# Counting four of sixteen key chunks earlier, adding six groups beside the slots, and two stores on another queue

## The chip, the cores and the metric

The kernel runs on one core of a Trainium2 chip. The metric is the device time of one execution in microseconds (us). The core has TensorE (PE, with its weight loads as PEld), VectorE (DVE), ScalarE (ACT), GpSimd (POOL) and SyncE (SP), each with its own queue of instructions that it works off in order; DMAs are issued from such a queue.

## The reference

Two layers work on 8192 nodes (128 graphs of 64) with 256 features.

```
x = x + L0_gnn(layernorm(x), adj)     # softplus(xn @ W_self + (I - A_norm) @ xn @ W_neigh)
x = x + L0_ffn(layernorm(x))          # H = gelu(xf @ W1 + b1): 8192 x 1024
                                      # probs = softmax(H @ Wg + bg); e = argmax(probs)
                                      # out = probs[e] * (H @ Wd[e] + bd[e]): one of 8 experts per node
x = x + L1_gnn(layernorm(x), adj)     # attention in each graph, layernorm, gelu
x = x + L1_ffn(layernorm(x), edges)   # messages over 1048576 edges give scores; two of 4 experts per node
```

The edge list's indices run up to 65536, but there are only 8192 nodes: a source past the last node is read as the last node, and edges whose target is past the last node do not count. So most edges that count have the last node as source, and for these it is enough to know how many go to each node (`cnt`). The others are collected as keys and handled one by one.

## The kernel before

Nodes lie in 64 tiles of 128; four tiles make a group (`GR`), two groups a part (`PART`). The program is written as generators: each `yield` ends a step, and `mix` (L168) interleaves several generators by the share of their steps that is done. A planner puts the instructions on the engines' queues by its own model of their times, with the written order as priority; so an instruction without a wait can be placed long before the place where it is written. `tc.issue_after(i)` keeps instructions behind `i` on its engine.

**Gate stage** (loop over i = 0 to 9 at L935 on). Streams of part i: `factors`, `graph` (layer 0's graph for two groups, i < 8), `gated` (L707; layer 0's hidden layer, the gate and the choice of an expert for two groups, i >= 2) and `keys.collect` (L259; for some chunks of 512 edges per partition it takes the largest keys with MAX8 and MATCH_REPLACE8 on DVE and stores the rest to `left`). `gated` sends each node's row of the hidden layer to `hrows`, sorted by expert, with indirect DMAs from GpSimd (L800). At i = 9 `early_table` finds eight tiles of `hrows` that are already full.

**Early slots** (`early_slots`, L859). For those eight tiles SP loads the hidden rows, PE transposes them and multiplies by the expert's weights `wd` (L914), DVE adds the bias (L922), and SP stores the result to `yrows` (L923). `slot_tables` (L978) is stepped beside them; it gives the tables by which the next stage finds its tiles.

**Slots** (`slots`, L1162; the loop at L1273 on). 60 further tiles are done in the same manner: `hin` loaded by SP (L1194), eight transposes to `th` (L1203), copied to `hTt` by ACT (L1206), sixteen matmuls to `py` (L1221), bias on DVE (L1229), store by SP (L1230). Each slot also steps three generators, issued after the slot before:

- `count` (L306): for a chunk's 96 keys per partition DVE splits the bits (`pi`, `pb`: L314, L316), makes one-hots for 16 keys (`HK`) with `pairs_equal` (L201; 128 and 64 wide, bf16), and PE sums their products in `cnt_ps`, one matmul per key (L326). Sixteen chunks of six steps make 96 steps.
- `finish` (L335): DVE finds each list's inner edges and writes the sorted keys (`own`, `pieces`, `key_tile`, `key_row`).
- `back_first` (L1139): for the first four groups (`FIRST` = 2 * `PART`) GpSimd gathers a tile's rows of `yrows` as soon as they are all stored (L1149), DVE adds them to `x` and takes the statistics (L1156, L1157), and `factors_of` makes the factors of the layernorm.

What is left of the three generators runs after the last slot, and then a branch (L1285) jumps over four further slots that these inputs do not need.

**Graph stage of layer 1** (loop over s = 4 to 25, L1604). In step s `back(s)` (L1434) gathers and adds group s like `back_first`, `first(s - 4)` starts a group's attention (z on ACT or DVE at L1329 and L1331, transposes at L1471), `second`, `combine` and `tables` follow some steps later, and from the later steps on units of the last feed-forward (`dense`) are put between.

Memory pools of one stage are laid over those of the stage before; a new tile waits for the old tile's last reader.

Of the kernel before, what the change touches and what calls it, by code (L numbers as in the profile page):

```python
# [21 lines left out]
P = 128  # L22
# [10 lines left out]
NSLOT = 72  # L33
SURE = 68
EARLY = 8
EPS = 1e-5
NEG = -9000000000000000.0
HALVES = (slice(0, 64), slice(64, 128))
# [44 lines left out]
def kernel(  # L83
# [113 lines left out]
    def pairs_equal(pool, numbers, of, k, n, name):  # L197
# [8 lines left out]
        )  # L206
        return o

    sorted_keys = {}
    facs = {}  # L210

# [14 lines left out]
    class Keys:  # L226
# [76 lines left out]
                keys.rearrange("p (n e) -> p n e", e=PER),  # L303
            )

        def count(self):  # L306

            behind = []
            for c in range(n_chunks):
                bits = self.slots.bitcast(I32)[:, c * KEPT : c * KEPT + KEPT]  # L310
                part = []
                for op, by, off in ((ALU.bitwise_and, P - 1, 0.0), (ALU.logical_shift_right, 7, -float(KEY >> 7))):
                    pi = self.work.tile([P, KEPT], I32, name="pi")
                    V.tensor_scalar(pi, bits, by, None, op)  # L314
                    pb = self.work.tile([P, KEPT], BF16, name=f"pb{by}")
                    V.tensor_scalar(pb, pi, off, None, ALU.add)  # L316
                    part.append(pb)
                for g in range(0, KEPT, HK):
                    one = []
                    for wi, pb, n in ((self.iota[0], part[0], P), (self.iota[1], part[1], NT)):  # L320
                        one.append(pairs_equal(self.twice, wi, pb[:, g : g + HK], HK, n, f"one{n}"))
                    behind.append((c * KEPT + g, one))
                    yield
                    at, one = behind.pop(0)
                    for k in range(HK):
                        nc.tensor.matmul(  # L326
                            self.ps,
                            one[0][:, k // 2, :, k % 2],
                            one[1][:, k // 2, :, k % 2],
                            start=(at + k == 0),  # L330
                            stop=(at + k == n_chunks * KEPT - 1),
                        )
            V.tensor_copy(cnt, self.ps)

        def finish(self, pool):  # L335

# [100 lines left out]
    with tc.tile_pool(name="w0", bufs=1, reuse_waits="tile") as w0, tc.tile_pool(name="kp", bufs=1, reuse_waits="tile") as kp:  # L437
# [30 lines left out]
        with tc.tile_pool(name="bg1", bufs=1, reuse_waits="tile") as bg1, tc.tile_pool(  # L468
# [19 lines left out]
            with tc.tile_pool(name="b2", bufs=1, reuse_waits="tile") as b2, tc.tile_pool(  # L488
# [370 lines left out]
                def early_slots():  # L859

                    _, rows_at = nc.values_load_multi_w_load_instructions(
                        early_row,
                        engines=(mybir.EngineType.SP,),
                        min_val=0,
                        max_val=E0 * N - P,
                        skip_runtime_bounds_check_because=why,
                    )
                    _, ex = nc.values_load_multi_w_load_instructions(
                        early_e,
                        engines=(mybir.EngineType.SP, mybir.EngineType.PE),  # L870
                        min_val=0,
                        max_val=E0 - 1,
                        skip_runtime_bounds_check_because=why,
                    )
# [24 lines left out]
                    load(1)  # L899
                    turn(0)  # L900
                    yield
                    for t in range(EARLY):
                        if t + 2 < EARLY:
                            load(t + 2)
                        if t + 2 == EARLY:
                            y_last = bh.tile([P, GR * P], F32, name="hT")[:, 0:D]
                        if t + 1 < EARLY:
                            turn(t + 1)
                        hT = turned_.pop(t)
                        bd = b2.tile([P, D], F32, name=f"z{2 + t % 2}")  # L910
# [12 lines left out]
                        nc.sync.dma_start(yrows[(NSLOT + t) * P : (NSLOT + t + 1) * P, :], y)  # L923
                        yield

                next_found(-1)
# [8 lines left out]
                for i in range(n_parts + 2):  # L935
# [25 lines left out]
                    if i >= 2:  # L961
                        with tc.issue_after(gelus[-1]) if gelus else ExitStack():
                            for at in islice(zeros, 2):
# [1 line left out]
                                    yrows[at : at + 8 * P, :].rearrange("(p r) (k f) -> p (r k) f", r=8, f=P),  # L965
                                    none.unsqueeze(1).to_broadcast([P, 8 * D // P, P]),
                                )
                    cs = [next(chunks) for _ in range((0, 1, 1, 2, 1, 2, 1, 2, 3, 3)[i])]
                    if cs:
                        streams.append((chain(*map(keys.collect, cs)), 8 * len(cs)))  # L970
                    if i == n_parts + 1:
                        streams.append((early_table(), 8))
                    mix(streams)
# [134 lines left out]
                early = early_slots()  # L1108
                for _ in early:
                    next(tables, None)  # L1110
                for _ in tables:
                    pass

        keep = ctx.enter_context(tc.tile_pool(name="keep", bufs=1, side="right", reuse_waits="tile"))
        sorted_keys["pieces"] = keep.tile([P, NB, PL, NPC], BF16, name="pieces")
# [3 lines left out]
        if True:  # L1119
            with tc.tile_pool(name="bs", bufs=3, reuse_waits="tile") as bs, tc.tile_pool(  # L1120
# [10 lines left out]
                keys.ps = psl.tile([P, NT], F32, name="cnt_ps")  # L1131
                steps, counts = keys.finish(bm), keys.count()
                stores, gathers = [], []

                def apart(made, others):
# [2 lines left out]

                def back_first():  # L1139

                    fac = None
                    for t in range(FIRST * GR):
                        i = t % (PART * GR)
                        if i == 0:
                            raw, fac = raws1[t // (PART * GR)], facs[t // (PART * GR)]
# [5 lines left out]
                        )  # L1151
                        gathers.append(got.ins)
                        apart(got, stores[t + E0 :])
                        for _ in range(3):
                            yield
                        V.scalar_tensor_tensor(x[:, t, :], y, psel[:, t : t + 1], x[:, t, :], ALU.mult, ALU.add)  # L1156
                        V.bn_stats(raw[:, 0, i, :], x[:, t, :])  # L1157
                        if i == PART * GR - 1:
                            yield
                            facs["last"] = factors_of(raw, None, [m[:, None, :] for m in mfs], fac)  # L1160

                def slots(first, end):  # L1162

# [100 lines left out]
                        )  # L1264
                    yield

                raws1 = [c0.tile([P, 1, PART * GR, 6], F32, name=f"raw_{i}") for i in range(FIRST // PART)]
# [4 lines left out]
                for t, unit in enumerate(slots(0, SURE - EARLY)):  # L1272
                    done = t  # L1273
                    with tc.issue_after(last) if last is not None else ExitStack():
                        next(back_early, None)
                        next(counts, None)
                        next(counts if t % 2 else steps, None)
                    if t >= SURE - EARLY - 8:
                        next(more, None)
                    last = unit  # L1280
# [129 lines left out]
    with ExitStack() as of_c:  # L1410
# [193 lines left out]
        for s in range(FIRST, n_steps):  # L1604
            if s % PART == 0:
                made["raw"] = c2.tile([P, 3, PART * GR, 6], F32, name="raw")
                made["eps"] = c2.tile([P, 3, PART * GR], F32, name="eps")
                V.memset(made["raw"], 0.0)
                V.memset(made["eps"], EPS)
            streams = []  # L1610
            for of, by_steps in ((back, 0), (combine, COMBINE), (tables, TABLES), (second, SECOND), (first, FIRST)):
                if 0 <= s - by_steps < NG:
                    streams.append((of(s - by_steps), 2 if of == second and s % 2 else 0))
            if s == TABLES + 1:
                with tc.issue_after(made["sent"]):
# [822 lines left out]
```

## Time and profile before

| | us |
|---|---|
| median of 3 runs | 2006.49 (2000.83 to 2007.28) |
| the profiled execution | 2002.07 |
| its span, first to last instruction | 2000.4 |
| PE busy (10609 matmuls) | 1875.0 (94%) |
| DVE busy | 1345.0 (67%) |
| ACT busy | 949.7 (47%) |
| POOL busy | 447.0 (22%) |

All times of the profile count from the span's start. In its tables a line gives the kernel's line, the engine, the operation and the tiles (written <- read). A wait names the engine and line whose end released the waiting instruction, with its total, the number of times and the longest. The mean granted clock of TensorE was 0.977 of full speed.

The stages lie so: gate to 616, early slots to 655, slots from 663 to 969, graph stage of layer 1 from 987 to about 1340, edges and the last feed-forward after it.

### The profile page before, as it was taken

To read this page: it belongs to the slowest core of one execution; us is meant where nothing else is said; L and a number is where in the kernel's file an instruction comes from. 1 tells how busy PE (TensorE), PEld (TensorE's weight loads), DVE (VectorE), ACT (ScalarE), POOL (GpSimd) and SP (SyncE) were. 2 spreads that over 40 slices of the span, in tenths; PEclk is the share of its full clock that TensorE was granted. 3 is DMA by queue.
4 is the path that set the end of the run, shared out by engine and by line. 5 is a ranking of instruction groups with operands and counts; after the bars stand their busy time and mean duration, and the time that the engine had idled before them with its cause. 6 is when DMAs were issued, how large, how long until landed. Compare 5 with 4: busy or idle time off the path is not lost. (4 is left out here: it accounts for less than half of the span.)

```text
span 2000.4 us, 32559 instructions
## 1 busy us (share of the span) xinstructions
PE 1875.0 (94%) x10609; PEld 1334.1 (67%) x10609; DVE 1345.0 (67%) x4421; ACT 949.7 (47%) x1740; POOL 447.0 (22%) x465
## 2 busy tenths in 40 slices
PE   7898999989999899999787999998999989999999
PEld 5444454544447899898654766665777758888876
DVE  6789988872224788999898775766788552334435
ACT  4867667676663121222277677432343423433332
POOL 2010111011110011100232100014677643313223
PEclk9999999999999999999897999998999999999999
DMA  9752322323425455554214211382322258888832
GB/s 295 209 164 81 119 83 97 109 90 113 157 94 170 166 169 172 167 163 144 69 53 158 76 50 53 111 246 67 74 51 68 83 178 286 286 250 280 278 122 95
DMA packets 243743, 284.91 MB, mean 142 GB/s; under 512 B 55920, under 2 KB 195568, under 8 KB 243568
## 3 DMA queue, kind: packets, MB, share of 16 engines
q1 hardware_dynamic: 209680, 222.22, 35.4%
q0 software_dynamic: 23040, 60.22, 9.2%
q8 instruction: 90, 1.47, 0.3%
q10 hardware_dynamic: 10848, 0.30, 0.3%
q14 instruction: 85, 0.70, 0.1%
HBM read 159.40 MB, written 123.18 MB: 141 GB/s over the span
## 5 line engine op out<-in xcount | busy, mean ns | idle before, releaser
L480 PE MATMUL ph<-zT,w 128*128 128x512 f32 x512 | 250.2, 613 | 4.2 <-ACT zT L729 3.2
L1221 PE MATMUL py<-wd,hTt 128*128 x960 | 217.6, 380 | 0.0
L1221 PEld LDWEIGHTS py<-wd,hTt 128*128 128x128 f32 x960 | 178.1, 191 | 22.6 <-issue 0.8
L1832 POOL DMA_INDIRECT got<-tsrc,esrc x144 | 156.1, 1084 | 157.6 <-DMA zslots<-none 75.6
L1206 ACT COPY hTt<-th 128x512 f32<-128x512 f32 x120 | 64.6, 589 | 248.0 <-PE th L1203 248.0
L1371 PE MATMUL py<-w,hT 128*128 128x256 f32 x736 | 173.3, 388 | 8.1 <-DVE kt L1771 4.7
L1361 PE MATMUL ph<-zT,w 128*128 128x512 f32 x368 | 168.1, 599 | 0.0
L480 PEld LDWEIGHTS ph<-zT,w 128*128 128x128 f32 x512 | 94.2, 196 | 107.0 <-issue 87.6
L1371 PEld LDWEIGHTS py<-w,hT 128*128 128x128 f32 x736 | 138.6, 193 | 34.2 <-issue 10.4
L2317 ACT ACTIVATE hT<-ph,b1e 128x256 f32<-128x256 f32 x152 | 72.1, 474 | 177.7 <-PE ph L2313 97.3
L2313 PE MATMUL ph<-zTp,w1e 128*128 128x256 f32 x608 | 139.3, 383 | 4.4 <-DMA w1e<-in_L_ffn_W_dram 4.4
L1365 ACT ACTIVATE hT<-ph,b 128x512 f32<-128x512 f32 x92 | 63.1, 688 | 163.3 <-PE ph L1361 161.6
L800 POOL DMA_INDIRECT hrows<-rows,pos x64 | 64.5, 1007 | 333.7 <-issue 160.4
L2334 DVE TENSOR_TENSOR y<-py,b2e 128x256 f32<-128x256 f32 x76 | 32.2, 424 | 158.6 <-PE py L2326 153.4
L2326 PE MATMUL py<-w,hT 128*128 x608 | 137.5, 379 | 0.0
L2313 PEld LDWEIGHTS ph<-zTp,w1e 128*128 128x128 f32 x608 | 116.7, 192 | 20.7 <-issue 4.6
L642 PE MATMUL pre<-wd 128*128 128x512 f32 x256 | 125.4, 607 | 1.9 <-ACT wd L628 1.3
L483 ACT ACTIVATE hT<-ph,b 128x512 f32<-128x512 f32 x128 | 88.1, 688 | 74.1 <-PE ph L480 72.5
L2326 PEld LDWEIGHTS py<-w,hT 128*128 128x128 f32 x608 | 112.6, 190 | 13.8
L201 DVE TENSOR_TENSOR one<-iota_l,pb 128x2048 bf16<-128x2048 bf16 x96 | 116.6, 1214 | 0.0
L1361 PEld LDWEIGHTS ph<-zT,w 128*128 128x128 f32 x368 | 67.2, 190 | 66.9 <-issue 66.0
L2347 POOL DMA_INDIRECT back<-yslots,place x64 | 65.2, 1019 | 165.9 <-ACT yb L1387 48.9
(486 smaller groups left out, 3799.6 us busy)
## 6 DMA issues: line engine op xcount, KB each, us to landing
hin<-hrows SPq DMA_DIRECT2D x60, 512.0 KB
w1e<-in_L_ffn_W_dram SPq DMA_DIRECT2D x38, 512.0 KB
yin<-ystore SPq DMA_DIRECT2D x24, 512.0 KB
yrows<-none SPq DMA_DIRECT2D x10, 1024.0 KB
zslots<-none SPq DMA_DIRECT2D x38, 256.0 KB
zin<-zslots SPq DMA_DIRECT2D x38, 256.0 KB
yslots<-y SPq DMA_DIRECT2D x76, 128.0 KB
ystore<-y SPq DMA_DIRECT2D x72, 128.0 KB
```

The costliest lines, as they stand in the source:

```text
L201: V.tensor_tensor(o, numbers.unsqueeze(1).to_broadcast(shape), of.rearrange("p (j e) -> p j e", e=2).unsqueeze(2).to_broadcast(shape), ALU ...
L480: nc.tensor.matmul(ph, w1[:, c, q * P : q * P + P], zT[:, c, :], start=(c == 0), stop=(c == 1))
L483: gelus.append(S.activation(hT, ph, AF.Gelu, bias=b1[:, q : q + 1]).ins)
L642: nc.tensor.matmul(pre, xnT[:, c, n * P : n * P + P], wcat[:, c, :], start=(c == 0), stop=(c == 1),)
L1221: nc.tensor.matmul(py, hT[:, q, :], wd[:, bass.ds(e, 1), q, :].rearrange("p e f -> p (e f)"), start=(q == 0), stop=(q == NH - 1),)
L1361: nc.tensor.matmul(ph, w1[:, e, c, q * P : q * P + P], zT[:, c, :], start=(c == 0), stop=(c == 1))
L1371: nc.tensor.matmul(py, hTs[q][:, k * P : k * P + P], w2[:, e, q, :], start=(q == 0), stop=(q == NH1 - 1))
L1832: nc.gpsimd.indirect_dma_start(got, None, tsrc, bass.IndirectOffsetOnAxis(ap=esrc[:, b, at : at + 1], axis=0))
L2313: nc.tensor.matmul(ph, w1e[:, c, q * P : q * P + P], zT[:, c, :], start=(c == 0), stop=(c == 1))
L2317: pace[:] = [S, S.activation(hT, ph, AF.Gelu, bias=b1e[:, q : q + 1]).ins]
L2326: nc.tensor.matmul(py, hTs[q][:, k * P : k * P + P], w2[:, e, q, :].rearrange("p e f -> p (e f)"), start=(q == 0), stop=(q == NH1 - 1),)
L2347: nc.gpsimd.indirect_dma_start(got[n], None, yslots[h], bass.IndirectOffsetOnAxis(ap=place[h][:, j, t : t + 1], axis=0))
```

## The change

- `count` takes a range of chunks, the number of keys in a step and its PSUM tile. Chunks 0 to 3 (`COUNTED`) are counted in steps of 8 keys (`HE`) as a stream of the gate stage at i = 8 and 9 (18 steps in each) and beside the early slots (two steps for each early tile). Their working tiles are carved (`Carved`) from those of `collect` and from factors no longer used. The other 12 chunks are counted in the slots as before, and the two sums are added. Bits are split in two halves of 48 keys, in a smaller tile `pi`.
- The collects are written earlier: 0, 1, 2, 2, 2, 3, 3, 3 chunks in parts 0 to 7 and none after, where it was 0, 1, 1, 2, 1, 2, 1, 2, 3, 3.
- In the slots `count` gets five steps in four slots (six before), `finish` five in eight (four before).
- `back_first` adds six groups (`BACKED`), with two steps for a tile in place of three; the addition comes one tile behind the gather. The graph stage's `back` skips groups 4 and 5, and copies their statistics.
- The last two of the eight early stores are issued by GpSimd.

```diff
+BACKED = 3 * PART
+COUNTED, HE = 4, 8
...
-        def count(self):
-            behind = []
-            for c in range(n_chunks):
+        def count(self, cs, hk, ps):
+            first, end = cs[0] * KEPT, (cs[-1] + 1) * KEPT
+            for c in cs:
...
-                    pi = self.work.tile([P, KEPT], I32, name="pi")
-                    V.tensor_scalar(pi, bits, by, None, op)
                     pb = self.work.tile([P, KEPT], BF16, name=f"pb{by}")
-                    V.tensor_scalar(pb, pi, off, None, ALU.add)
+                    for g in range(0, KEPT, KEPT // 2):
+                        pi = self.work.tile([P, KEPT // 2], I32, name="pi")
+                        V.tensor_scalar(pi, bits[:, g : g + KEPT // 2], by, None, op)
+                        V.tensor_scalar(pb[:, g : g + KEPT // 2], pi, off, None, ALU.add)
...
-                for g in range(0, KEPT, HK):
+                for g in range(0, KEPT, hk):
...
-            V.tensor_copy(cnt, self.ps)
+            if first:
+                V.tensor_tensor(cnt, cnt, ps, ALU.add)
+            else:
+                V.tensor_copy(cnt, ps)
...
-                        nc.sync.dma_start(yrows[(NSLOT + t) * P : (NSLOT + t + 1) * P, :], y)
+                        queue = nc.sync if t < EARLY - 2 else nc.gpsimd
+                        queue.dma_start(yrows[(NSLOT + t) * P : (NSLOT + t + 1) * P, :], y)
...
-                    cs = [next(chunks) for _ in range((0, 1, 1, 2, 1, 2, 1, 2, 3, 3)[i])]
+                    cs = [next(chunks) for _ in range((0, 1, 2, 2, 2, 3, 3, 3, 0, 0)[i])]
...
+                    if i == n_parts:
+                        l, r = (keys.work.tile([P, CHUNK], I32, name=n).bitcast(BF16) for n in ("src", "dst"))
+                        m = keys.work.tile([P, CHUNK + PER], F32, name="key").bitcast(BF16)
+                        n = HE * NT
+                        keys.work = keys.twice = Carved(
+                            one128=(l, r),
+                            one64=(m[:, 0:n], m[:, n : 2 * n]),
...
+                            pi=(gone[:, P : P + KEPT // 2].bitcast(I32),),
+                        )
+                        counts = keys.count(range(COUNTED), HE, psa.tile([P, 2 * D], F32, name="pre")[:, 0:NT])
+                    if i >= n_parts:
+                        n = COUNTED * (KEPT // HE) * 3 // 8
+                        streams.append((islice(counts, n), n))
...
                 for _ in early:
                     next(tables, None)
-                for _ in tables:
-                    pass
+                    next(counts, None)
+                    next(counts, None)
+                for of in (tables, counts):
+                    for _ in of:
+                        pass
...
-                steps, counts = keys.finish(bm), keys.count()
+                steps = keys.finish(bm)
+                counts = keys.count(range(COUNTED, n_chunks), HK, psl.tile([P, NT], F32, name="cnt_ps"))
...
-                    for t in range(FIRST * GR):
+                    for t in range(BACKED * GR):
...
-                        for _ in range(3):
-                            yield
-                        V.scalar_tensor_tensor(x[:, t, :], y, psel[:, t : t + 1], x[:, t, :], ALU.mult, ALU.add)
-                        V.bn_stats(raw[:, 0, i, :], x[:, t, :])
+                        yield
+                        if held:
+                            add()
+                        held.append((t, y))
+                        yield
...
-                        next(counts if t % 2 else steps, None)
+                        next(steps if t % 2 == 0 or t % 8 == 3 else counts if t % 4 == 1 else iter(()), None)
...
+                if s < BACKED:
+                    V.tensor_copy(made["raw"][:, 0], raws1[s // PART][:, 0])
...
-                if 0 <= s - by_steps < NG:
+                if 0 <= s - by_steps < NG and (of != back or s >= BACKED):
```

More of the change, by code (lines that the diff above doesn't have):

```diff
@@ L207, in pairs_equal, with __init__, tile @@
         return o
+    class Carved:
+        def __init__(self, **views):
+            self.views, self.at = views, dict.fromkeys(views, 0)
+        def tile(self, shape, dtype, name):
+            views = self.views[name]
+            self.at[name] += 1
+            view = views[self.at[name] % len(views)]
+            if len(shape) == 4:
+                return view.rearrange("p (j n e) -> p j n e", n=shape[2], e=2)
+            return view
     sorted_keys = {}
@@ L312, in count @@
                 for op, by, off in ((ALU.bitwise_and, P - 1, 0.0), (ALU.logical_shift_right, 7, -float(KEY >> 7))):
-                    pi = self.work.tile([P, KEPT], I32, name="pi")
-                    V.tensor_scalar(pi, bits, by, None, op)
                     pb = self.work.tile([P, KEPT], BF16, name=f"pb{by}")
-                    V.tensor_scalar(pb, pi, off, None, ALU.add)
+                    for g in range(0, KEPT, KEPT // 2):
+                        pi = self.work.tile([P, KEPT // 2], I32, name="pi")
+                        V.tensor_scalar(pi, bits[:, g : g + KEPT // 2], by, None, op)
+                        V.tensor_scalar(pb[:, g : g + KEPT // 2], pi, off, None, ALU.add)
                     part.append(pb)
-                for g in range(0, KEPT, HK):
+                for g in range(0, KEPT, hk):
                     one = []
                     for wi, pb, n in ((self.iota[0], part[0], P), (self.iota[1], part[1], NT)):
-                        one.append(pairs_equal(self.twice, wi, pb[:, g : g + HK], HK, n, f"one{n}"))
-                    behind.append((c * KEPT + g, one))
+                        one.append(pairs_equal(self.twice, wi, pb[:, g : g + hk], hk, n, f"one{n}"))
                     yield
-                    at, one = behind.pop(0)
-                    for k in range(HK):
+                    at = c * KEPT + g
+                    for k in range(hk):
                         nc.tensor.matmul(
-                            self.ps,
+                            ps,
                             one[0][:, k // 2, :, k % 2],
                             one[1][:, k // 2, :, k % 2],
-                            start=(at + k == 0),
-                            stop=(at + k == n_chunks * KEPT - 1),
-                        )
-            V.tensor_copy(cnt, self.ps)
+                            start=(at + k == first),
+                            stop=(at + k == end - 1),
+                        )
+            if first:
+                V.tensor_tensor(cnt, cnt, ps, ALU.add)
+            else:
+                V.tensor_copy(cnt, ps)
         def finish(self, pool):
@@ L967 @@
                                 )
-                    cs = [next(chunks) for _ in range((0, 1, 1, 2, 1, 2, 1, 2, 3, 3)[i])]
+                    cs = [next(chunks) for _ in range((0, 1, 2, 2, 2, 3, 3, 3, 0, 0)[i])]
                     if cs:
                         streams.append((chain(*map(keys.collect, cs)), 8 * len(cs)))
+                    if i == n_parts:
[5 more added lines that the diff above has]
+                            one64=(m[:, 0:n], m[:, n : 2 * n]),
+                            pb127=(m[:, 2 * n : 2 * n + KEPT],),
+                            pb7=(m[:, 2 * n + KEPT : 2 * n + 2 * KEPT],),
+                            pi=(gone[:, P : P + KEPT // 2].bitcast(I32),),
[4 more added lines that the diff above has]
+                        streams.append((islice(counts, n), n))
                     if i == n_parts + 1:
@@ L1130 @@
                 keys.psum, psl = pool("psp", 1, space=PSUM), pool("psl", 1, space=PSUM)
-                keys.ps = psl.tile([P, NT], F32, name="cnt_ps")
-                steps, counts = keys.finish(bm), keys.count()
+                steps = keys.finish(bm)
+                counts = keys.count(range(COUNTED, n_chunks), HK, psl.tile([P, NT], F32, name="cnt_ps"))
                 stores, gathers = [], []
@@ L1139, in back_first, with add @@
                 def back_first():
-                    fac = None
-                    for t in range(FIRST * GR):
-                        i = t % (PART * GR)
-                        if i == 0:
-                            raw, fac = raws1[t // (PART * GR)], facs[t // (PART * GR)]
+                    held = []
+                    def add():
+                        t, y = held.pop()
+                        i, part = t % (PART * GR), t // (PART * GR)
+                        raw = raws1[part]
+                        V.scalar_tensor_tensor(x[:, t, :], y, psel[:, t : t + 1], x[:, t, :], ALU.mult, ALU.add)
+                        V.bn_stats(raw[:, 0, i, :], x[:, t, :])
+                        if i == PART * GR - 1 and part in facs:
+                            facs["last"] = factors_of(raw, None, [m[:, None, :] for m in mfs], facs[part])
+                    for t in range(BACKED * GR):
                         while done < t + E0 - 1:
@@ L1153, in back_first @@
                         apart(got, stores[t + E0 :])
-                        for _ in range(3):
-                            yield
-                        V.scalar_tensor_tensor(x[:, t, :], y, psel[:, t : t + 1], x[:, t, :], ALU.mult, ALU.add)
-                        V.bn_stats(raw[:, 0, i, :], x[:, t, :])
-                        if i == PART * GR - 1:
-                            yield
-                            facs["last"] = factors_of(raw, None, [m[:, None, :] for m in mfs], fac)
+                        yield
[3 more added lines that the diff above has]
+                        yield
+                    yield
+                    add()
                 def slots(first, end):
@@ L1265, in weights @@
                     yield
-                raws1 = [c0.tile([P, 1, PART * GR, 6], F32, name=f"raw_{i}") for i in range(FIRST // PART)]
+                raws1 = [c0.tile([P, 1, PART * GR, 6], F32, name=f"raw_{i}") for i in range(BACKED // PART)]
                 for i in range(FIRST // PART):
```

## The prediction

> **What bounds the kernel now.** I read the page first for the shares, then the table of stages (busy time of each engine in chosen stretches), the order in time of PE, ACT, SP and DVE around the seams that the table shows, and last the waits there.
>
> ```profile
> span 2000.4 us, 32559 instructions
> 508.00:613.00 105.00, 96.58 (x400) 49.44 (x400) 24.42 (x129) 65.41 (x105) 15.93 (x16) 0.95 0.35 127
> ...
> 655.00:663.00 8.00, 3.14 (x15) 3.17 (x16) 6.94 (x30) 1.48 (x3) 0.00 (x0) 0.64 0.68 237
> 663.00:969.00 306.00, 303.72 (x2829) 273.01 (x2828) 272.74 (x627) 63.13 (x118) 25.22 (x16) 1.00 0.49 158
> 969.00:988.00 19.00, 8.07 (x144) 7.60 (x141) 18.51 (x39) 6.12 (x12) 2.46 (x1) 0.65 0.16 47
> 988.00:1020.00 32.00, 31.07 (x145) 21.48 (x143) 25.63 (x86) 18.37 (x44) 18.11 (x19) 0.94 0.24 71
> 1020.00:1060.00 40.00, 27.75 (x111) 18.06 (x110) 37.68 (x123) 28.62 (x52) 16.99 (x17) 0.83 0.19 56
> ```
>
> The columns after the length are busy PE, weight load, DVE, ACT and POOL, then granted clock, DMA share, GB/s. PE is full in the slots (663 to 969), and DVE with 272.7 of 306 close behind. In the gate's last groups (508 to 613) DVE works 24 of 105 us. Two holes are plain: 655 to 663, and 969 to 988, where DVE is full and PE works 8 of 19 us at a clock of 0.65. From 1020 to 1060 DVE (37.7 of 40) holds PE up again. From 1100 to 1300 PE has over 49 of every 50 us, so time won before it should last to the end.
>
> PE's order of time in the slots, at their end, and the waits from 940 to 1000:
>
> ```profile
> 667.15 1.04 PE L1203 MATMUL th<-ident,hin 128*128 128x128 f32 x8
> 668.02 3.62 PE L1221 MATMUL py<-wd,hTt 128*128 x16
> 671.48 1.13 PE L326 MATMUL cnt_ps<-one,one 128*128 128x64 bf16 x32
> ...
> 968.74 1.13 PE L326 MATMUL cnt_ps<-one,one 128*128 128x64 bf16 x32
> ...
> 986.67 1.01 PE L326 MATMUL cnt_ps<-one,one 128*128 128x64 bf16 x16 [0.73 <-DVE one L201]
> 987.49 1.95 PE L1471 MATMUL tz<-ident,z 128*128 128x128 f32 x8
> ...
> ACT z L1329 <- PEq L1285: 10.9, 1, 10.9
> ACT z L1329 <- DVE pieces L434: 8.4, 1, 8.4
> ```
>
> The last slot's matmuls end at 968.7; next comes counting, paced by DVE's one-hots, until 986.7, and only then the first transpose of the graph stage. Its input, ACT's z, waited for PE's branch and for DVE's last step of `finish`.
>
> SP's order at the other seam, and PE's row that waits there:
>
> ```profile
> 651.86 0.35 SPq L923 DMA_DIRECT2D yrows<-z  x1
> 655.36 0.35 SPq L923 DMA_DIRECT2D yrows<-hT  x1
> 656.54 1.41 SPq L1194 DMA_DIRECT2D hin<-hrows  x3
> ...
> 659.86 3.65 PE L1203 MATMUL th<-ident,hin 128*128 128x128 f32 x16 [5.04 <-DMA hin<-hrows]
> ```
>
> SP issues in order, so the slots' first loads stand behind the last early store, which waits for PE's last early tile.
>
> **The change, part by part.** Minus is time saved.
>
> *Counting moved.* 96 steps of 16 keys make 1536 matmuls; a quarter, 384, leaves. Two slots take 10.14 us (667.15 to 677.29) with 48 count matmuls; two pure slots are 2 x (0.87 + 3.46) = 8.66, so a count matmul costs 1.48/48 = 31 ns. Before, 1536 - 144 = 1392 (87 steps) lay in the slots; after, at most 72 steps do: 15 x 0.48 = **-7.2 us**. The 384 go beside the gate and the early slots as 48 steps of 8 keys: 384 x 31 ns = 11.9 us of PE. PE idles 8.4 of 105 us in 508 to 613, one wait of 1.4 us in each group (for ACT's row copies) among it; the planner can put counting there. I fill 4 us: **+7.5**, bounds +3 (all 8.4 filled) and +12. On DVE a step costs 0.68 (1024 elements, as the row of 128x1024) plus about 0.42 (512 elements, estimated on the line through 1214 ns for 2048 and 682 for 1024): 48 x 1.1 = 53 us. DVE is idle for 81 us in 508 to 613 and for 16 in 616 to 655, which hides it if the plan puts the one-hots ahead of their matmuls; the uncovered price is in the second rival. The collects were planned for later parts, yet the last MAX8 of a chunk ran at 428 us, so dealing them out earlier costs nothing (if DVE pushed the graph's work back there, up to +3).
>
> *The end of the slots.* Count steps are now offered 60 + 15 = 75 times in 60 slots, for 73 needed; `finish`, with some 33 steps, gets 38 places (30 before); the 24 gathered tiles need 7 + 2 x 24 = 55 slots. So all three should end inside. Does DVE hold it? From 655 to 988 it worked 6.9 + 272.7 + 18.5 = 298. Off: 24 steps at 1.75 (42) and four chunks of split bits (2). On: the split in halves of 12 chunks (6), eight more tiles at 0.47 + 0.42 less overlap (6.5). That is 267 of the 300 us or so from the last early tile to the end of the slots: 89%, as before, and at that share PE waited only 1.6 us for one-hots in the whole stage. What remains at 968.7 to 987.5 (18.7 us) is PE's branch, four z (2.1 us, 972.17 on) and the hand-over, some 3.5 us: **-15.2**, bounds -8 (half the tail stays) and -16.5.
>
> *Clock.* With the hole PE restarts slowly: eight transposes take 1.95 us at 987.49 and 1.09 at 995.94, eight matmuls of 257 columns 3.22 and 2.00. **-2** (0 to -3). [...]
>
> *Six groups beside the slots.* Eight tiles leave the graph stage: 8 x (0.47 + 0.42) = 7.1 us of DVE and eight gathers on POOL. DVE holds PE only from 1020 to 1060, where PE idles 12 us: I take **-4** (0 to -7). A copy of statistics comes on DVE, under 0.3 us.
>
> *Two stores to GpSimd.* SP is free after its last bias load at 648.06; register reads (0.8 us) and the three loads follow, and land by about 654, 3.3 us after issue as now. PE then goes on at 655 instead of 659.86 and skips part of the slow restart (3.65 for 16 transposes against 2 x 1.04). In exchange GpSimd's two stores land later than SP's: its nearest rows are gathers, 0.95 to 1.69 us of issue and 4.6 us to landing, and the first copy to hTt may wait for the buffer of the sixth store, about 0.5 us. POOL's queue is empty there until the first gather at 705. **-5** (-7 to +1).
>
> [...]
>
> *Sum:* -7.2 + 7.5 - 15.2 - 2 - 4 - 5 = -25.9. Against the profiled execution's 2002.1 us that is 1976.2; against the median shown, 2006.5 (4.4 above that execution), 1980.6. I put it halfway, 1978.
>
> **The rivals.**
> 1. *Part of the tail stays*: DVE falls behind in the slots, whose in-order queue is 89% full, and `finish` or the counts run past the last slot. For: PE waits for one-hots at 947 and 959, when the weights' few steps come on top. Price: half of the 18.7 us and PE stalls of 2: 1978 + 10 = 1988.
> 2. *The gate pays (slower)*: PE's queue is in order, so a count matmul planned too early for its one-hot stops all gate matmuls behind it. A step fully exposed costs 1.1 us, 48 of them 53, in place of the +7.5: 2004 - 33 (the sum without the +7.5) + 12 + 53 = 2036. It decides from (26 + 6)/48 = 0.67 us of stall a step. Against it: DVE is 77% idle there, two pairs of buffers let it run ahead, and in the slots a DVE three times as busy did not stop PE.
> 3. *Given back later*: the graph stage starts 26 us earlier but is held by its own chain (z, exp, ring on ACT and DVE, PE 27.8 of 40 us) and the replanned order is worse by as much: no change, 2004. Against: PE is full from 1100, so only a 100 us stretch could swallow it.
> 4. *The stores do nothing*: the loads still wait, for a buffer instead of SP. Then the -5 becomes 0: 1983, inside the forecast's range.
>
> **How the numbers follow.** Forecast (with the fourth) 0.63, first rival 0.17, second 0.10, third 0.10. The forecast's own range from the bounds, not all met at once, is 1966 to 1992. The first rival lies within it and up to 1998, where I put the end; the slow case and most of "given back" stay outside. A measurement here can tell about 0.3% (6 us) from no change. Faster 0.81 (forecast and first rival with a little of the third), same 0.08, slower 0.11.
>
> **What would show it.** Right: count matmuls (form 128x64, bf16) between 500 and 655, none after the last slot's py; under 5 us from that py to the first graph transpose, and no stretch there at 0.65 clock; hin issued before the last early y; 5 count steps in each 4 slots; 40 gathers in the graph stage. Wrong: PE waits for DVE's one-hots between 500 and 655 of over 10 us in all, group periods in the gate over 30 us (25 now, 2 more expected), `finish` steps after the last py, or a longer stretch from the first graph transpose to 1100's full PE.

## The result, and the profile after

The changed kernel takes 1975.58 us (median of 6 runs, 1971.18 to 1977.13); the kernel before, in 6 runs beside them, 2003.05 us (2000.42 to 2007.28). The ratio is 0.9856, with a 95% interval of 0.9839 to 0.9874: faster by 1.4%. The forecast was 1978. The profiled execution took 1972.22 us with a span of 1970.5, against 2002.07 and 2000.4 before.

The table of stages of the changed kernel (start and end, length, then busy PE, weight load, DVE, ACT and POOL, the granted clock, DMA share, GB/s):

```profile
508.00:613.00 105.00, 98.26 (x656) 56.07 (x655) 52.81 (x210) 65.46 (x105) 16.42 (x16) 1.00 0.35 128
657.00:660.40 3.40, 2.16 (x17) 1.75 (x17) 3.04 (x19) 0.67 (x2) 0.63 (x1) 1.00 0.97 368
660.40:959.00 298.60, 295.50 (x2577) 264.87 (x2577) 266.83 (x669) 63.66 (x119) 38.97 (x24) 1.00 0.52 167
959.00:961.00 2.00, 1.01 (x6) 0.47 (x6) 0.97 (x4) 1.71 (x4) 0.00 (x0) 1.00 0.22 70
960.05:992.05 32.00, 30.44 (x145) 20.53 (x146) 20.03 (x74) 23.24 (x55) 11.14 (x12) 1.00 0.20 55
992.00:1032.00 40.00, 26.87 (x113) 17.36 (x111) 38.32 (x126) 29.72 (x54) 17.95 (x17) 0.83 0.20 60
```

Three things are to be seen. In the same 105 us of the gate PE now holds 656 instructions in place of 400, yet is busy for 1.7 us more, and its granted clock is 1.00, not 0.95. The two holes (8 and 19 us, clock 0.64 and 0.65) have shrunk to 3.4 and 2 us. In the graph stage DVE is relieved in the first 32 us (20.0 against 25.6), where PE was nearly full already, and not at all in the next 40 (38.3 against 37.7), where it holds PE up.

PE's order of time in a gate group of the kernel before, where it waits for ACT's rows:

```profile
564.87 1.79 PE L728 MATMUL tz<-ident,z 128*128 128x128 f32 x8 [1.36 <-ACT rows L738]
```

And in the same place of the changed kernel, and behind its slots (the early one-hots lie in tiles carved from `key`, `src` and `dst`, and their sums in a `pre` tile of PSUM):

```profile
562.20 0.40 PE L341 MATMUL pre<-key,src 128*128 128x64 bf16 x8
562.44 0.40 PE L341 MATMUL pre<-key,dst 128*128 128x64 bf16 x8
563.72 0.44 PE L746 MATMUL tz<-ident,z 128*128 128x128 f32 x2 [0.88 <-ACT rows L756]
564.00 0.40 PE L341 MATMUL pre<-key,src 128*128 128x64 bf16 x8
...
960.05 1.81 PE L1515 MATMUL tz<-ident,z 128*128 128x128 f32 x8 [0.94 <-DVEq L1329]
962.43 2.00 PE L1526 MATMUL pw<-wx,zT 128*128 128x257 f32 x8 [0.57 <-ACT zT L1516]
```

A step of eight count matmuls (L341) takes 0.40 us, and steps stand where PE used to wait 1.36 us for ACT's rows; 0.88 of that wait is left. The last slot's matmuls end at 959.1 and the first graph transpose starts at 960.05; the eight matmuls of 257 columns behind it take 2.00 us (3.22 before).

SP's and POOL's queues at the other seam:

```profile
650.82 0.35 SPq L942 DMA_DIRECT2D yrows<-z  x1
651.36 0.33 SPq L929 DMA_DIRECT2D z<-in_L_ffn_bd_dram  x1
652.56 1.37 SPq L1238 DMA_DIRECT2D hin<-hrows  x3
```

```profile
654.08 0.60 POOL L942 DMA_DIRECT2D yrows<-z  x1 [26.29 <-DVE z L940]
657.59 0.63 POOL L942 DMA_DIRECT2D yrows<-hT  x1 [2.90 <-DVE pi L331]
```

The slots' loads (`hin`) are issued at 652.56, ahead of both last early stores; before, they came at 656.54, behind them.

Cut into stretches from one row's start to the next, the 29.9 us of span went as follows:

| stretch | before | after | saved (-) | forecast |
|---|---|---|---|---|
| start to last gate matmul `ms` | 610.7 | 610.4 | -0.3 | +7.5 with the next |
| to the last early `py` | 43.7 | 46.0 | +2.2 | |
| to the first slot's `py` | 8.9 | 4.0 | -4.9 | -5 |
| to the last slot's `py` | 305.2 | 298.4 | -6.9 | -7.2 |
| to the first graph transpose | 19.0 | 1.3 | -17.6 | -15.2 |
| to the first dense matmul | 104.0 | 102.2 | -1.7 | -4 and -2 |
| to the end of the span | 908.9 | 908.2 | -0.7 | 0 |

### The profile page after: what moved, and what is told of

Same layout as the page of the kernel before. It is cut to its first block, busy times and chain, and to the rows that moved or that the text cites. A ratio compares the mean times of both kernels' runs of the same rounds, so it can differ in the third digit from the quotient of the medians.

```text
span 1970.5 us, 32697 instructions
## 1 busy us (share of the span) xinstructions
PE 1860.5 (94%) x10609; PEld 1323.8 (67%) x10609; DVE 1354.6 (69%) x4535; ACT 947.9 (48%) x1740; POOL 453.9 (23%) x467
## 5 line engine op out<-in xcount | busy, mean ns | idle before, releaser
L755 PEld LDWEIGHTS tz<-ident,hT 128*128 128x128 f32 x512 | 62.2, 143 | 52.6 <-issue 42.2
```

## The experiments

Twelve kernels ran, in three groups of four, each group on one chip; the changed kernel and the one before are among them again as e0 and e8. The chips of the first and the third group took 2040.8 and 2033.9 us for the kernel before, so what is compared is each kernel's ratio to runs of the kernel before on its own chip, and the stretches. The stretches are of one profile each. From the first dense matmul to the end the profiles have 907 to 909 us on the chip of before and after and on the second, but 928 to 944 on the other two, by no order that the edits explain; so there the ratios can't tell effects of a few us apart. In the table, "gate" is the time from the first gate matmul of the 12th group to that of the 16th (a gate matmul is an `ms` with the weights `wg`); the rest are the stretches above.

| kernel | ratio (95%) | gate | to early py | to slot py | slots | to graph | to dense |
|---|---|---|---|---|---|---|---|
| before | 1 | 106.4 | 43.7 | 8.9 | 305.2 | 19.0 | 104.0 |
| after | 0.9856 | 106.7 | 46.0 | 4.0 | 298.4 | 1.3 | 102.2 |
| *first chip* | | | | | | | |
| e1 stores on SP | 0.9833 (0.9803-0.9863) | 106.7 | 46.8 | 8.8 | 300.0 | 1.3 | 106.0 |
| e2 four groups | 0.9869 (0.9835-0.9904) | 106.7 | 47.3 | 4.1 | 297.3 | 1.3 | 111.7 |
| e3 count in slots | 0.9932 (0.9913-0.9952) | 104.7 | 46.3 | 3.6 | 304.0 | 20.5 | 102.2 |
| e4 counted twice | 0.9874 (0.9841-0.9907) | 109.7 | 52.3 | 3.1 | 298.5 | 1.3 | 105.8 |
| *second chip* | | | | | | | |
| e0 control | 0.9867 (0.9852-0.9882) | 106.7 | 46.0 | 4.4 | 300.0 | 1.3 | 103.6 |
| e8 before again | 1.0 (0.9991-1.0009) | 106.1 | 43.0 | 8.9 | 304.9 | 19.0 | 103.6 |
| e6 one in eight | 0.9842 (0.9828-0.9855) | 104.6 | 43.4 | 3.7 | 298.5 | 1.3 | 104.7 |
| e7 six chunks | 0.986 (0.9843-0.9877) | 113.8 | 47.1 | 3.9 | 288.7 | 1.3 | 103.4 |
| *third chip* | | | | | | | |
| e5 late finish | 0.9854 (0.9833-0.9876) | 106.7 | 46.5 | 4.0 | 294.8 | 4.0 | 105.3 |
| e9 eight groups | 0.9864 (0.984-0.9887) | 106.7 | 46.7 | 4.0 | 301.6 | 1.3 | 106.6 |
| e10 eight, six chunks | 0.9856 (0.9833-0.988) | 115.5 | 49.3 | 4.1 | 289.2 | 1.3 | 109.4 |
| e11 four again | 0.9884 (0.9856-0.9911) | 106.7 | 46.7 | 4.2 | 297.3 | 1.3 | 111.9 |

**The stores on SP again.**

```
- queue = nc.sync if t < EARLY - 2 else nc.gpsimd
+ queue = nc.sync
```

> The changed kernel with all eight early stores on SP again. My theory (SP's order holds the slots' first loads): the first slot's py starts some 8.5 us after the end of the last early py instead of 3.6, everything behind it comes 5 us later, about 1980.5 us (ratio to before 0.988). Rival (the loads wait for a buffer, or the hole closes for another reason): the stretch stays at 3.6 us and the time at 1975.6.

The gap is back: 8.8 us from the last early `py` to the first slot's, where the kernels with the stores as changed have 3.1 to 4.4 on every chip. SP's queue, and PE's wait in 655 to 670:

```profile
660.87 0.35 SPq L942 DMA_DIRECT2D yrows<-hT  x1
662.04 1.41 SPq L1238 DMA_DIRECT2D hin<-hrows  x3
...
PE th L1247 <- DMA hin<-hrows: 5.2, 1, 5.2
```

The loads stand behind the last early store again, and PE waits 5.2 us for them. That the order on SP's queue was the cause, and no buffer, is shown. The time does not show it: the ratio expected was 0.988, and 0.9833 came, with an interval 12 us wide that overlaps the changed kernel's.

**Four groups beside the slots, twice** (e2 on the first chip, e11 on the third; the same kernel).

```
- BACKED = 3 * PART
+ BACKED = 2 * PART
```

> The changed kernel with only four groups added beside the slots; groups 4 and 5 are back in the graph stage. My theory after the two traces: the eight tiles were taken from a stretch in which DVE was not the limit, so giving them back costs 0 to 2 us (1976 to 1977.6); DVE works about 25 us of the graph stage's first 32 instead of 20, and the stretch behind it, where DVE is full, keeps its length. Rival (the prediction's term): DVE holds PE there, so the time rises by 4 to 7 us, to 1980 to 1983.

> Four groups again (BACKED = 2 * PART), with everything else as changed, for a row on the same chip as eight groups. Theory (without the hole each group moved is worth some 2.5 us): first graph transpose to first dense matmul 108 to 112 us, ratio 0.003 above the control's 0.9867. Rival (the 111.7 us belonged to the other chip): 103 to 106 us and the control's ratio.

The stretch up to the first dense matmul is 111.7 and 111.9 us, against 106.0 and 105.8 with six groups on the first chip: the two groups are worth 5.8 us there. Some of it is paid in the slots, 298.5 to 300.0 with six and 297.3 with four. So my theory (0 to 2 us) fell for that stretch and the rival, the prediction's own term, held; the ratios are too wide to show it. The groups do work, though the pair of traces has only 1.7 us. What hid them is the subject of the next two experiments.

**All counting in the slots.** The gate's counting is left out of the plan, and `count` runs over all 16 chunks beside the slots, with `count` and `finish` stepped in the order of the kernel before; stores and six groups stay as changed.

```
- counts = keys.count(range(COUNTED, n_chunks), HK,
+ counts = keys.count(range(n_chunks), HK,
- next(steps if t % 2 == 0 or t % 8 == 3 else counts if t % 4 == 1 else iter(()), None)
+ next(counts if t % 2 else steps, None)
```

> The changed kernel with all sixteen chunks counted in the slots, in the order of steps of the kernel before; the stores and the six groups stay. My theory (the tail of counting and finish was most of the loss): the slots grow by 7 us, the hole between the last slot's py and the first graph transpose is 18 us or more again, the gate wins 2 us; about 2000 us (1996 to 2006). Rival (stores, groups and an easier graph stage carry the gain): 1985 to 1992.

The hole is back, 20.5 us, and the slots take 304.0. The time is another matter: 0.9932 of the kernel before is 1989 us on the chip of before and after, in the rival's range and not in the theory's 1996 to 2006. So the early counting carries about half of the gain, some 15 us; the other 14 or so fall to the stores, the six groups and the collects, which the ratios don't tell apart. The stretch behind the hole is *shorter*: 102.2 against 105.9 us without a hole (e1, e4), with the same six groups on the same chip. A head start for the graph stage is not the only reading of these 3.7 us. In e1 and e4 the first eight matmuls of 257 columns take 3.60 and 3.67 us and in e3 2.18, which makes 1.4 to 1.5 of them (e5 has the granted clock beside them in two profiles); and the two kernels with six groups and no hole in which they take 2.00 us, the changed one (102.2) and e7 (103.4), are about as short as e3.

**The control and the kernel before on one chip.** No edit.

> The changed kernel unmodified, as a control on the chip that runs the next three and, if it is the same chip, the four before. Theory (the seams are the same on any chip, only late parts differ in absolute time): last early py within 2 us of 655 to 658, under 5 us from its end to the first slot py, under 2 us from the last slot py to the first graph transpose; ratio to the kernel before 0.985 +- 0.003, so that the runs with one part undone lie 0 (stores), 0 to 0.003 (groups) and 0.006 to 0.012 (counting) above it. Rival (the gain belongs to one chip): ratio over 0.99 here.

> The kernel before, unmodified, for its trace on the same chip. It closes a square with three other kernels: four or six groups beside the slots, with or without the hole of 19 us ahead of the graph stage. Measured is the stretch from the first graph transpose to the first dense matmul of the first weight matrix. Theory (the hole was also a head start: the graph stage's first gathers and its DVE work went ahead in it, so without the hole the stretch is longer by about 4 us, and the six groups shorten it by about 4 to 6): this kernel some 4 us shorter than four groups without the hole (111.7 us), so 106 to 108. Rival (no head start; the groups alone differ): within 1 us of 111.7.

The control's ratio, 0.9867, repeats the result. The stretch of the kernel before is 103.6 us, the same as the control's: on this chip two more groups and a closed hole gave nothing there in all. It lies below the 106 to 108 expected, and 8 us below the four groups without a hole on the other chips, so the rival (no head start) is further off. DVE's order in the graph stage's first microseconds shows what the head start is, first in the kernel before (its first transpose is at 988.8), then in e11 (961.3):

```profile
989.58 0.46 DVE L1455 SCALAR_TENSOR_TENSOR x<-yin,psel,x 128x256 f32<-128x256 f32 x1
```

```profile
969.40 0.48 DVE L1499 SCALAR_TENSOR_TENSOR x<-yin,psel,x 128x256 f32<-128x256 f32 x1 [6.33 <-DMA yin<-yrows,row_y]
```

And POOL's first gather of the graph stage, in the same two kernels:

```profile
982.16 2.46 POOL L1440 DMA_INDIRECT yin<-yrows,row_y  x1 [62.34 <-DVE one L201]
```

```profile
965.40 0.95 POOL L1484 DMA_INDIRECT yin<-yrows,row_y  x1 [118.10 <-PE pw L1526]
```

With the hole the first gather goes out 6.6 us ahead of the first transpose and DVE adds its row without a wait (the next rows cost it 2.9 us). Without it the gather goes out 4.1 us behind, and DVE stands 6.33 us. So with four groups closing the hole takes away a head start: 103.6 us with it (e8), 111.7 and 111.9 without (e2, e11), 8.2 us between chips. With six groups DVE needs no gathered row until 983.5 in the control, 19.5 us after the first transpose, and has no such wait; there 1.4 to 1.5 of the 3.7 us of e3 lie in the first eight matmuls of 257 columns, and how much of the rest is a head start stays open. So the two extra groups pay for what closing the hole costs: +8.2 and -5.8 (e2 against e1 and e4) make +2.4, and the two pairs of before and after have -1.7 and 0.0. Since chips differ by up to 3.8 us in this stretch, the sum is no closer than that.

**One early count matmul in eight.** Of every eight count matmuls beside the gate and the early slots only the first is issued: 48 in place of 384, so the counts are incomplete; the one-hots are all made.

```
- for k in range(hk):
+ for k in range(0, hk, 8 if hk == HE else 1):
```

> Of each step of eight counted keys beside the gate and the early slots only one matmul is issued, so 336 of the 384 early count matmuls are left out and the counts are incomplete. One-hots and all else stay. Theory (the early matmuls fill pockets in which PE waited, and so cost little): the last gate matmul ends within 1 us of the control, the last early slot 1 to 3 us earlier, the whole run 1 to 4 us faster. The granted clock of the gate's last 105 us falls back from 1.00 towards 0.95. Rival (each costs its 31 ns): early slots end 10 us earlier, the run 10 us faster than the control.

Gate and early slots lose 2.1 and 2.6 us against the control, 4.7 for 336 matmuls: 14 ns each, less than half of the 31 of a full queue. The theory had it too cheap: the last gate matmul comes 2.6 us earlier and not within 1, the last early `py` 5.3 us earlier and not 1 to 3. The clock falls only to 0.98, not to 0.95. e3, which counts nothing early, gives a lower price: against e1 and e2 it saves 2.0 us in the gate and 0.5 to 1.0 in the early slots for all 384, but at a clock of 0.89 in the early slots, where e1 and e2 have 1.00. In e6 the two stretches are 147.9 us, 1.1 less than in the kernel before (149.0), so something else in the change, perhaps the collects dealt out earlier, gives a little back. That was not tried alone.

**The early matmuls doubled.** Each count matmul beside the gate and the early slots is issued a second time, into a second PSUM tile that nobody reads, from the same one-hots.

```
+ if twin is not None:
+     nc.tensor.matmul(twin, one[0][:, k // 2, :, k % 2], one[1][:, k // 2, :, k % 2], ...)
```

> The changed kernel with each count matmul beside the gate and the early slots issued twice, the second into a PSUM tile that nobody reads. My theory (the first 384 fell into PE's idle pockets and kept its clock up, and little of the pockets is left): the second 384 cost 6 to 12 us, the last early py ends 6 to 12 us later and the time is 1982 to 1988. Rival (small matmuls between the large ones cost nearly nothing): 0 to 4 us, 1976 to 1980.

Gate +3.0 us, early slots +5.0 to +5.5 against e2 and e1: some 8.3 us, 22 ns for each of 384, as the theory had it. The ratio (0.9841 to 0.9907) can't tell it from the rival. The first 384 found more room than the second. The gate's last 105 us and the early slots of this kernel:

```profile
508.00:613.00 105.00, 102.32 (x888) 61.64 (x890) 52.59 (x210) 64.42 (x103) 16.26 (x16) 1.00 0.34 124
613.80:666.50 52.70, 49.92 (x511) 44.06 (x504) 36.83 (x155) 13.12 (x23) 4.46 (x5) 0.97 0.54 184
```

PE is busy for 102.3 of 105 us in the gate, where the changed kernel has 98.3 and the one before 96.6: the pockets are nearly full.

**Six chunks early.**

```
- COUNTED, HE = 4, 8
+ COUNTED, HE = 6, 8
- counts if t % 4 == 1
+ counts if t % 12 == 1
```

> Six of the 16 chunks counted early in place of four: 192 more matmuls beside the gate and the early slots, 12 steps of 16 fewer in the slots (the extra places for counting go from 18 to 6). Theory (the gate's pockets are mostly filled: PE idles 6.7 of its last 105 us): early slots end 3 to 6 us later than the control's, the slots take 5.8 us less (192 x 31 ns), the end of the slots unchanged: within 3 us of the control. Rival (the pockets hold these too): 4 to 6 us faster. Rival (DVE can't make 24 more pairs of one-hots in time, and PE waits for them): over 5 us slower.

Within 3 us of the control, as the theory said, but from two larger parts: gate and early slots +8.3 us (expected 3 to 6), slots -11.3 (expected -5.8). In the slots 3.8 us of PE's waits for one-hots and for `hTt`, which the control still has, fall away besides. 192 more matmuls cost 43 ns each beside the gate, twice those of e4, which need no new one-hots. PE's longest entry from 505 to 670:

```profile
PE pre L341 <- DVE key L203: 4.6, 7, 1.0
```

The control has 1.4 us there. These waits are 3.2 of the 8.3 us. That is the beginning of the second rival, a gate that waits for one-hots, at half as many chunks again; four chunks stay well under it.

**`finish` late.**

```
- next(steps if t % 2 == 0 or t % 8 == 3 else counts
+ next(steps if t % 2 == 0 else counts
```

> finish gets a step in every even slot only, 30 places as before the change, in place of 38; all else as changed. Theory (the hole ahead of the graph stage was DVE work left over after the last slot, whichever it was): finish's last 3 steps or so stand on DVE behind the last slot's y, 5 to 7 us of DVE work; the last slot py to the first graph transpose takes 5 to 8 us in place of 1.4, z waits for pieces, granted clock below 1.00 there, and the ratio is 0.002 to 0.003 above the control's. Rival (the hole was counting's alone, since PE's queue held the matmuls): under 2 us there and the ratio of the control, 0.985 to 0.988.

The hole grows to 4.0 us, less than the 5 to 8 expected, and the slots take 294.8 us, 2.5 less than in e11, the next shortest on this chip with four chunks early. Slots and hole together, 298.8 us, are no longer than e11's 298.6: the late steps only moved from one to the other. In the end its ratio, expected 0.002 to 0.003 above the control's, can't be told from it. PE behind the slots:

```profile
960.01 1.06 PE L1515 MATMUL tz<-ident,z 128*128 128x128 f32 x8 [3.65 <-DVEq L1329]
964.29 3.78 PE L1526 MATMUL pw<-wx,zT 128*128 128x257 f32 x8 [3.22 <-ACT zT L1516]
```

After 3.65 us idle the transposes keep their full pace (1.06 us); after 3.22 more the 257-column matmuls take 3.78 us. After 0.94 and 0.57 they took 2.00 in the changed kernel's profile, but 3.48 in the control's, with the same two waits ahead of them:

```profile
963.95 1.81 PE L1515 MATMUL tz<-ident,z 128*128 128x128 f32 x8 [0.94 <-DVEq L1329]
966.32 3.48 PE L1526 MATMUL pw<-wx,zT 128*128 128x257 f32 x8 [0.56 <-ACT zT L1516]
```

The granted clock differs with it. Two windows of 3.4 us in the control, then two in the changed kernel (columns as in the table of stages):

```profile
963.30:966.70 3.40, 2.08 (x10) 1.16 (x11) 1.59 (x10) 3.40 (x8) 0.00 (x0) 1.00 0.15 43
966.70:970.10 3.40, 3.40 (x9) 2.20 (x8) 0.00 (x0) 2.16 (x6) 1.91 (x2) 0.50 0.20 54
```

```profile
958.20:961.60 3.40, 2.35 (x13) 1.24 (x11) 1.57 (x7) 2.31 (x5) 0.00 (x0) 1.00 0.13 41
961.60:965.00 3.40, 2.83 (x13) 1.92 (x13) 0.27 (x5) 3.40 (x9) 0.95 (x1) 1.00 0.04 7
```

In the control the clock is at half from 966.7 to 970.1, over just these matmuls; in the changed kernel it stays full. The two are one kernel, so no edit made the 1.5 us between 2.00 and 3.48. In the clock records of the profiles of the kernel before and of the changed one, all 23 stretches at half clock that end within the span last 3.41 us or a whole multiple of it, hence the windows' width; the control's first one ends where its stretch begins, and the changed kernel's are counted back in such steps from its next stretch, at 999.1. In the control most of both waits lies in one window, with PE busy for 2.08 of 3.40 us; in the changed kernel each lies in one of its own, with 2.35 and 2.83. No run varied what lies ahead of these matmuls alone, so what decides between the two restarts is not shown. In e5 the mean clock from 960 to 992 is 0.89, against 1.00 in the changed kernel from 960.05 to 992.05.

**Eight groups, and eight groups with six chunks.** In both, one of the two waits for a slot falls away for every odd tile, so that 32 tiles fit; e10 adds e7's edit.

```
- BACKED = 3 * PART
+ BACKED = 4 * PART
-                        yield
+                        if t % 2 == 0:
+                            yield
```

> Eight groups in place of six are added beside the slots: 32 gathered tiles, three slots for each two tiles in place of two for each. Theory (DVE holds the first 70 us of the graph stage, so each group taken out of it gives about 2.5 us, as four against six groups did with 111.7 against 105.9 us on one chip): the stretch from the first graph transpose to the first dense matmul is 4 to 6 us shorter than with six (103.5 in the control), 97 to 100 us; the slots stay within 2 us of the control's 299.9, DVE at 91%; ratio 0.002 to 0.003 below the control's. Rival (the stretch is bound by the chain and not by DVE's load beyond six groups): within 1.5 us of 103.5. Rival (the slots' DVE is over-full): slots over 304 us or a hole over 4 us ahead of the graph stage, no gain.

> The eight groups of the run before and six chunks counted early as in the earlier run, which leaves DVE 246 + 7 of 289 us in the slots. Theory (both add up): early slots end 7 to 9 us later than with four chunks, slots 289 us (299.9), first transpose to first dense matmul 97 to 100 us: ratio 0.980 to 0.985, the fastest of these kernels. Rival (six groups is where the graph stage stops gaining): 0.985 to 0.987.

My theory fell: 106.6 and 109.4 us up to the first dense matmul in place of 97 to 100. DVE's first waits in that stretch of e9:

```profile
DVE x L1500 <- DMA yin<-yrows,row_y: 16.5, 6, 10.0
DVE x L1598 <- ACT z L1595: 5.5, 3, 3.1
```

DVE stands 16.5 us for gathered rows, which come later than their place in DVE's order; the load is gone and the wait has taken its place. In e10 the slots save as much as in e7 and the gate and this stretch take it back; its ratio, 0.9856, is the rival's and not the 0.980 to 0.985 expected. Within the intervals no kernel here is faster than the changed one and still computes everything.

## Why the prediction was right

The likeliest case came: 1978 was forecast and 1975.58 measured; in the forecast's own terms -25.9 us of the profiled execution against -29.85. That the sum came so near is in part luck: the gate's cost was put 5.5 us too high and the end of the slots saved 2.4 more than forecast, while the groups and the clock together saved 4.3 less.

*Counting moved.* The slots' -7.2 was -6.9 (-4.9 between control and e8). The +7.5 for the gate and the early slots was the most mis-sized term: +2.0 in the pair and +2.2 between e8 and the control, from the start to the last early `py`. I let 4 of 11.9 us vanish in PE's pockets; e6 shows that 336 matmuls cost 4.7 of their 10.4 us, so more than half vanish, and the gate's group period, forecast to grow by 2 us from 25, stays at 26.7 (106.7 / 4; it was 26.6 and not 25 before). The clock has a part in it, which the term left out: in the gate's last 105 us three stretches of 3.4 us at half clock (the 0.95) are gone.

*The end of the slots.* -17.6 for -15.2. DVE held, at 266.8 of 298.6 us, 89% as worked out, and both `finish` and counting ended inside. What was too large was the hand-over, put at 3.5 us: PE waits 0.94 us in all; ACT's first z starts at 959.29, 0.2 us after the last slot's matmuls, and the transposes start behind the first z and not behind all four, so 1.3 us is left. e3 brings the hole back and e5 a part of it, by the same cause: work queued on DVE and PE behind the last slot.

*Clock.* The restart goes from 3.22 to 2.00 us in the changed kernel's profile (-1.2 for the -2) but not in the control's (3.48), so the term lies between +0.3 and -1.2. Both are profiles of one kernel, with the same two waits of PE (0.94 us, then 0.56 or 0.57) ahead of these matmuls and a clock of 0.50 over them in the control alone. That the changed kernel's profile had the faster restart is luck.

*Six groups.* The -4 was argued from DVE's load in 1020 to 1060. The step that failed is "eight tiles leave the graph stage, and DVE holds PE there": the relief fell into the first 32 us, and in the pair only -1.7 is left of this term and the clock's together. e2, e8 and e11 give the reason: the groups are worth 5.8 us when the hole is closed, but with four groups closing the hole costs some 8 us of head start (between chips), which no term of mine had. It is a piece of the third rival (given back later), at some 8 us in place of 26, and the two groups bought it back.

*Two stores.* -5 forecast, -4.9 in the pair, and e1 takes it back (8.8 us, PE waiting 5.2 for `hin`). On GpSimd the two stores take 0.60 and 0.63 us of issue against SP's 0.35. PE did not wait for them, and DVE once, 0.6 us for the last one's landing, at no cost to the seam.

Rival one (part of the tail stays) and rival four (the stores do nothing) are refuted by 1.3 and 4.0 us at the two seams. Rival two (the gate pays) needs 0.67 us of stall a step; PE's waits for early one-hots in the changed kernel are 1.4 us in all 48 steps, and 0.9 more ahead of weight loads.

## What to carry to other kernels

Work that one engine does in a seam, while the others stand, is best dealt out into an earlier stage where both of its engines have pockets; price it below its full-queue duration (here 31 ns a matmul), and find by doubling it how much more the pockets hold (here 14 ns, then 22, and 43 once new operands had to be made as well). Before counting a hole as pure loss, look for what is issued ahead in it: gathers and loads that the next stage needs first lose their head start when the hole closes (here some 8 us), and something must cover for them. An in-order DMA queue that mixes late stores with the next stage's first loads is worth splitting, even onto a queue that issues more slowly (here 0.60 and 0.63 us against 0.35, and the seam went from 8.9 to 4.0 us).

## What the runs showed of the hardware that was not expected

- In the gate's last 105 us, with waits of at most 1.4 us each, the granted clock was 0.95 in both profiles of the kernel before and 0.97 in e3; with count matmuls in them it was 1.00, and 0.98 with an eighth of these matmuls.
- The same idle times of PE (0.94 and 0.56 or 0.57 us) ahead of the same eight matmuls were followed by 2.00 us in six kernels (after, e2, e7, e9, e10, e11) and by 3.48 to 3.67 us in three (control, e1, e4). In the control the clock was 0.50 from 966.7 to 970.1, over these matmuls; in the changed kernel it was 1.00 from 958.2 to 965.0.
- In e3 the clock in the early slots (609 to 656.5 us) was 0.89, and 0.96 and 1.00 in the two profiles of the kernel before, though none of them counts there. Each is one profile.
